# Attention stage of a two-block network: denominators spread through memory, VectorE's convolution taps shared out, the last pair's convolution mostly on TensorE

## The chip, the cores and the metric

The kernel runs on one core of one Trainium2 chip. The core has five engines that run their own queues in order: TensorE (PE, with its weight loads shown as PEld), VectorE (DVE), ScalarE (ACT), GpSimd (POOL) and SyncE (SP), which here only issues DMAs. The metric is device time of one execution in microseconds (us); lower is better. Time before the change: 3925.6 us, the median of 3 runs (3922.62 to 3926.04).

## The reference, cut to what matters

The first block replaces three convolutions by table look-ups with a softmax over 16 centroids; it is not touched by the change. The second block is what the change is about: a group norm, a linear attention with rotary positions, and a depthwise 3x3 convolution ("lepe") that is added to it.

```python
x = relu(L0(x))                      # (32, 1024, 14, 14): look-up convolutions, not touched
y = group_norm(x, G=32)
# _L1_conv_ref(y): 16 heads of 64 channels, n = 14*14
q = elu(Wq @ y[:, :512] + bq) + 1
k = elu(Wk @ y[:, 512:] + bk) + 1
q_rope, k_rope = rope(q), rope(k)
km = k.mean(over n)
z  = 1 / (einsum('bhdn,bhd->bhn', q, km) + 1e-6)          # the denominators
kv = s * s * einsum('bhdn,bhen->bhde', k_rope, y)
attn = einsum('bhdn,bhde->bhne', q_rope, kv) * z
lepe = depthwise_conv3x3(y, lepe_w) + lepe_b
out  = x + attn + lepe
```

## The kernel before, in words

**Stages.** Three look-up layers fill the first 2660 us of the execution. Then the attention stage runs over 16 pairs of images (NP = 16; a pair is 392 positions, N2). All of the change lies in this stage.

**How a pair is worked.** Channels are cut into eight tiles of 128 (c = 0 to 7; half h = 0 is c = 0 to 3, for the queries, h = 1 is c = 4 to 7, for the keys). For each half, `load` brings x and the third layer's output by SP; `front` finishes the first block's output on ACT and DVE (L1124, L1133, L1138) and takes statistics (L1143); `group_norm` averages them on PE (L1165) and makes scales on POOL; `normalise` writes y on ACT, padded to 15 columns so that shifted windows can be read, and then turns x in place into x plus the centre tap and bias of the convolution (both L1218). `channels` multiplies y with the weights on PE (L1250) and makes elu + 1 on ACT (L1259, L1262) and DVE (L1267 queries, L1271 keys). `rope` turns queries and keys on POOL (L1291 to L1298). `tokens` transposes y and keys on PE (L1309) and copies them out on ACT (L1312); `products` makes kv on PE (L1346) and masks it on DVE (L1355).

**Denominators.** `normalisers` makes q times mean k on PE (L1397, 32 columns to each head group) and the inverse z on DVE (L1406, L1407). Then, four times a pair, `normalise_q` spreads four rows of z over 128 partitions with a matmul by a selection matrix (L1418), ACT copies the result to `zb` (L1424), and POOL multiplies the turned queries with it (L1421).

**Output.** For each of four head groups (n = 0 to 3, j = 2, 3, 0, 1; two channel tiles each), `attend` multiplies queries and kv on PE into two PSUM banks `pa` (L1438). `lepe` then adds the eight outer taps of the convolution onto each bank on DVE, one instruction a tap (L1455), and adds the bank onto x (L1469). After two head groups `store` writes a half of the output (L1478). There are eight banks: four `mm`, three `pa`, one `w`.

**Order.** The order of every engine's queue is written out by a planner (`Plan`). Each piece of work is given an engine, a rank (its due time), a weight (its cost in us), what it reads and writes, and a lag until its result can be used. `write` simulates time: an engine that is free takes, of the pieces whose inputs are done and whose buffers are free, the one of lowest rank. The order that comes out is fixed; on the chip an engine waits at a piece whose input is late, and what is behind it waits too. Buffers are `Slot`s that go round in rings in order. The ranks of pair p are offset by t = 80 p, and the attention and taps of a pair are ranked one T = 80 later, so that they fall beside the products of the next pair.

Of the kernel before, what the change touches and what calls it, by code (L numbers as in the profile page):

```python
# [10 lines left out]
F32 = mybir.dt.float32  # L11
# [30 lines left out]
class Slot:  # L42


    def __init__(self, pool, make):
        self.pool, self.make, self.ap, self.left = pool, make, None, 0
# [5 lines left out]
class Plan:  # L52
# [9 lines left out]
    def __init__(self, bufs):  # L62
        self.pieces, self.last, self.read = [], {}, {}
        self.ring = {n: [None] * k for n, k in bufs.items()}
# [19 lines left out]
    def write(self):  # L84
# [9 lines left out]
        nexts = {n: 0 for n in self.ring}  # L94
# [7 lines left out]
        def roomy(slots):  # L102
            take = {}
            for s in slots:
                if s.ap is None:
                    ring = self.ring[s.pool]
                    k = take.get(s.pool, nexts[s.pool])
                    old = ring[k % len(ring)]
                    if old is not None and old.left:
                        return False  # L110
                    take[s.pool] = k + 1
            return True

        while events:
            now, _, done = heapq.heappop(events)
            if done is not None:
                for m in after[done]:
                    count[m] -= 1
                    if count[m] == 0:
                        heapq.heappush(ready[self.pieces[m][0]], (self.pieces[m][1], m))  # L120
                for s in self.pieces[done][5]:
                    s.left -= 1
            if events and events[0][0] <= now:
                continue
            for e in engines:
# [17 lines left out]
                for s in slots:  # L143
                    if s.ap is None:
                        ring = self.ring[s.pool]
                        ring[nexts[s.pool] % len(ring)] = s
                        nexts[s.pool] += 1
                        s.ap = s.make()
# [12 lines left out]
def conv_preact_kernel(ctx: ExitStack, tc: tile.TileContext, a: dict, out: bass.AP):  # L161
# [793 lines left out]
    with ExitStack() as s:  # L955

        once = s.enter_context(tc.tile_pool(name="p4c", bufs=1))
        xp = s.enter_context(tc.tile_pool(name="p4x", bufs=5))
        p2 = s.enter_context(tc.tile_pool(name="p4b", bufs=1))
        mm = s.enter_context(tc.tile_pool(name="ps_mm", bufs=4, space=PSUM))  # L960
        pap = s.enter_context(tc.tile_pool(name="ps_pa", bufs=3, space=PSUM))
        wp = s.enter_context(tc.tile_pool(name="ps_w", bufs=1, space=PSUM))
# [50 lines left out]
        ph = mm.tile([P, 512], F32, tag="mm", name="ph")[:, :P]  # L1013
# [41 lines left out]
        bufs = dict(x=5, o3q=2, e=2, k=2, q=4, qr=5, ks=2, zb=2, mm=4, pa=3, w=1)  # L1055
        bufs |= {f"{n}{h}": 1 for n in ("vt", "kt") for h in range(2)}
        bufs |= {f"kv{i}{jp}": 1 for i in range(2) for jp in range(2)}
        plan = Plan(bufs)
        do = plan.do
        PE, DVE, ACT, POOL, SP = "PE", "DVE", "ACT", "POOL", "SP"  # L1060

        def slot(pool, shape, space=None):
            return Slot(
                pool,
                lambda: (space or p2).tile(shape, F32, tag=pool, name=pool, bufs=bufs[pool]),
            )

        bank = lambda pool: slot(pool, [P, 512], {"mm": mm, "pa": pap, "w": wp}[pool])
# [18 lines left out]
        def load(p, h, rank):  # L1087

            xt = slot("x", [P, 4, N2])
# [12 lines left out]
            for k in range(2):  # L1102
                ot = slot("o3q", [P, 2, N2])
# [9 lines left out]
        def front(p, h, c, xt, ot, rank):  # L1113

            ch = 4 * h + c
            w = bank("w")
# [34 lines left out]
        def group_norm(p, h, rank):  # L1151
# [7 lines left out]
            pm, pv = bank("mm"), bank("mm")  # L1159
# [11 lines left out]
            def centred():  # L1171
                for t in (g("gd"), pd()):
                    nc.vector.tensor_tensor(t, mean, bc(pm()[:, :8], 2, 2), ALU.subtract)
                nc.vector.tensor_tensor(g("gd"), g("gd"), pd(), ALU.mult)
                nc.vector.scalar_tensor_tensor(
                    g("gq"), m2, 1.0 / 98.0, g("gd"), ALU.mult, ALU.add
# [31 lines left out]
        def normalise(p, h, c, xt, rank):  # L1208
# [29 lines left out]
            do(ACT, rank + 24, 0.92, apply("xsc", "xbi", "x"), [key("xsc"), key("xbi")], [xk])  # L1238


        def channels(p, keys, j, r, t, sums, rank):
            w, first, b = (wk, 4, "kb") if keys else (wq, 0, "qb")
            pq, e = bank("mm"), slot("e", [P, N2])
# [33 lines left out]
            do(PE, rank, 2.76, product, ys_, [pq], lag=0.25)  # L1277
# [25 lines left out]
        def tokens(dst, dk, blocks, keys, rank):  # L1303

            pt = bank("mm")
# [5 lines left out]
            do(PE, rank, 0.5, turn, keys, [pt], lag=0.25)  # L1311
# [12 lines left out]
        def k_tokens(p, i, h, jp, kt, rank):  # L1324
# [4 lines left out]
                [("kr", 2 * jp + j) for j in range(2)],  # L1329
# [3 lines left out]
        def products(i, jp, kts, vts, rank):  # L1333

            pk = bank("mm")
            t = slot(f"kv{i}{jp}", [P, 2, 2, P])
# [37 lines left out]
        def normalisers(qs, ks, rank):  # L1374
# [16 lines left out]
            pd = bank("mm")  # L1391
# [16 lines left out]

            qk = [(q, r) for q in qs for r in range(2)]
            do(PE, rank, 2.3, piece, [*qk, ("kmm", 0), ("kmm", 1)], [pd], lag=0.25)  # L1410
            do(DVE, rank - 10, 3.0, inverse, [pd], ["z"])

        def normalise_q(j, qr, rank):
            pz, zb = bank("mm"), slot("zb", [P, N2])
            v = slice(32 * j, 32 * j + 32)

            def spread():
                nc.tensor.matmul(pz()[:, :N2], sel[v], z[v], start=True, stop=True)  # L1418
# [4 lines left out]
            do(PE, rank, 0.6, spread, ["z"], [pz], lag=0.25)  # L1423
            do(ACT, rank - 10, 0.48, lambda: nc.scalar.copy(zb(), pz()[:, :N2]), [pz], [zb])  # L1424
            do(POOL, rank, 1.65, times, [zb], [qr], port=True)

        def attend(j, kvs, qr, rank):


            pa = [bank("pa") for hp in range(2)]  # L1430

            def piece():
                for i in range(2):
                    for r in range(2):
                        for hp in range(2):
# [6 lines left out]
                                start=(r == 0),  # L1442
                                stop=(r == 1),
# [3 lines left out]
            return pa  # L1447

        def lepe(p, c, pa, xt, rank):


            def tap(k):
                def piece():
# [3 lines left out]
                        neighbours(p, c, 15 * (k // 3 - 1) + k % 3 - 1),  # L1457
# [13 lines left out]
            for n, k in enumerate([k for k in range(9) if k != 4]):  # L1471
                do(DVE, rank + n, 0.555, tap(k), [("y", p % 2, c)], [pa])
# [144 lines left out]
```

## Time and profile before

| | us |
|---|---|
| median of 3 runs | 3925.6 |
| profiled execution, its own time | 3921.16 |
| span of that execution | 3919.2 |
| first product of the attention stage (L1250) starts | 2712.5 |
| reciprocals of the denominators (L1407), mean period of the last 11 full pairs before the last | 72.5 |
| last reciprocal starts | 3858.49 |
| PE busy in the span | 3741.2 (95%) |
| DVE busy in the span | 3054.1 (78%) |
| mean granted clock of TensorE | 0.974 |

Each pair repeats the same pattern, so the reciprocal of its denominators marks its period: they start at 2990.17, 3060.87, 3134.89 and so on to 3787.66, and the stretches between them can be compared as windows. In a row of the windows, each engine's busy time stands with the number of its instructions, then the clock granted to TensorE (1 is full speed), and the share and rate of the DMA engines. What is left after the last reciprocal is a tail in which no further pair covers anything.

### The profile page before, as it was taken

The numbers are of one execution on the slowest core, as the hardware profiler recorded it, in microseconds if no ns is written. First come the engines' busy times: TensorE is split into PE (matmuls) and PEld (weight loads), VectorE is DVE, ScalarE is ACT, GpSimd is POOL, SyncE is SP. The second block draws the span as 40 slices with busy tenths as digits, with TensorE's granted clock in tenths as the row PEclk, the third lists the DMA queues.
The fourth block names the chain that finished last, engine by engine and source line by source line (L and its number), as shares of the span: only waits on it lengthen the run. The fifth ranks groups of instructions, "written<-read, shape, count | busy, mean of one in ns | idle before, by whom it ended". The sixth has DMA issues, their size and how long they took to land. (4 is left out here: it accounts for less than half of the span.)

```text
span 3919.2 us, 45921 instructions
## 1 busy us (share of the span) xinstructions
PE 3741.2 (95%) x16475; PEld 2097.3 (54%) x16475; DVE 3054.1 (78%) x4395; ACT 1664.6 (42%) x3797; POOL 2226.9 (57%) x1248
## 2 busy tenths in 40 slices
PE   8999999999999999999999999994999999999995
PEld 5555555544555455554444444442666666666664
DVE  8999999978888888888533333323799999999997
ACT  4555555533333333333222211213756666666661
POOL 7999999964444444444211111103877777777773
PEclk9999999999999999999999999997999999999997
DMA  3111111024333333432011110114122222222111
GB/s 114 34 34 33 34 33 32 2 74 104 83 69 87 69 83 69 97 73 60 32 38 38 38 38 19 38 38 135 42 67 62 71 71 63 67 71 75 55 54 34
DMA packets 209028, 228.13 MB, mean 58 GB/s; under 512 B 23888, under 2 KB 206672, under 8 KB 208792
## 3 DMA queue, kind: packets, MB, share of 16 engines
q1 hardware_dynamic: 208216, 224.96, 21.4%
q8 instruction: 133, 2.18, 0.2%
q14 instruction: 103, 0.84, 0.1%
q10 hardware_dynamic: 576, 0.15, 0.0%
HBM read 151.51 MB, written 73.55 MB: 57 GB/s over the span
## 5 line engine op out<-in xcount | busy, mean ns | idle before, releaser
L525 POOL TENSOR_TENSOR t<-t,r 128x1664 f32<-128x1664 f32 (+1 forms) x284 | 1064.2, 3747 | 1188.8 <-DVE r L524 1153.1
L558 PE MATMUL po<-t,lut 128*128 128x392 f32 x4096 | 1418.4, 500 | 0.5 <-POOL t L525 0.5
L558 PEld LDWEIGHTS po<-t,lut 128*128 128x128 f32 x4096 | 760.0, 190 | 627.0 <-issue 124.7
L487 ACT ACTIVATE t<-sc,cbias 128x392 f32<-128x392 f32 (+1 forms) x1136 | 579.8, 593 | 1034.8 <-PE sc L823 646.9
L1250 PE MATMUL mm<-y,qk 128*128 128x392 f32 x2048 | 727.1, 507 | 4.1 <-POOL xbi L1192 4.1
L909 PE MATMUL po<-t,lut 128*128 128x448 f32 x1792 | 680.3, 540 | 0.0
L499 DVE STREAM_TRANSPOSE tt<-t 128x1664 f32<-128x1664 f32 (+1 forms) x284 | 544.3, 1917 | 168.5 <-ACT t L487 168.5
L1455 DVE SCALAR_TENSOR_TENSOR pa<-y,lepe_w,pa 128x406 f32<-128x406 f32 x1024 | 607.1, 638 | 10.5 <-PE pa L1438 9.2
L524 DVE STREAM_TRANSPOSE r<-rc 128x1664 f32<-128x1664 f32 (+1 forms) x284 | 546.6, 1925 | 21.3 <-DVE rc L518 0.9
L1250 PEld LDWEIGHTS mm<-y,qk 128*128 128x128 f32 x2048 | 386.5, 194 | 283.9 <-issue 32.8
L909 PEld LDWEIGHTS po<-t,lut 128*128 128x128 f32 x1792 | 338.4, 190 | 339.9 <-issue 339.6
L918 DVE BATCH_NORM_STATS2 stats<-o 128x6 f32<-128x448 f32 x112 | 69.0, 617 | 488.4 <-ACT o L917 488.4
L516 DVE TENSOR_REDUCE sm<-tt 128x104 f32<-128x832 f32 (+2 forms) x284 | 423.1, 1490 | 5.4
L502 POOL TENSOR_TENSOR tt<-tt 128x832 f32<-128x832 f32 x128 | 248.1, 1938 | 7.8 <-DVE tt L499 7.8
L917 ACT COPY o<-po 128x448 f32<-128x448 f32 x112 | 59.0, 528 | 419.6 <-PE po L909 375.5
L518 DVE RECIPROCAL rc<-sm 128x104 f32<-128x104 f32 (+1 forms) x284 | 229.5, 808 | 9.8
L814 PE MATMUL sc<-patch,cw 64*128 64x392 f32 x1024 | 211.1, 520 | 4.7 <-DMA patch<-h1d 3.2
L1291 POOL TENSOR_TENSOR kr<-k,cosq 128x784 f32<-128x784 f32 x64 | 104.0, 1625 | 129.8 <-DVE k L1271 100.6
L1421 POOL TENSOR_TENSOR qr<-qr,zb 128x784 f32<-128x784 f32 x64 | 116.1, 1845 | 103.0 <-ACT zb L1424 103.0
L526 ACT ACTIVATE sm<-sm 128x104 f32<-128x104 f32 (+1 forms) x284 | 86.2, 304 | 174.6 <-DVE rc L518 174.6
L1124 ACT ACTIVATE w<-x,tb,gn_a 128x196 f32<-128x196 f32 x256 | 133.3, 521 | 58.5 <-DMA x<-in_x_dram 33.9
L814 PEld LDWEIGHTS sc<-patch,cw 64*128 64x128 f32 x1024 | 90.5, 186 | 116.5 <-issue 73.4
(156 smaller groups left out, 3844.6 us busy)
## 6 DMA issues: line engine op xcount, KB each, us to landing
patch<-h1d SPq DMA_DIRECT2D x248, 162.8 KB
x<-in_x_dram SPq DMA_DIRECT2D x32, 784.0 KB
o3d<-o SPq DMA_DIRECT2D x14, 1792.0 KB
x<-in_x_dram SPq DMA_DIRECT2D x64, 392.0 KB
o3q<-o3d SPq DMA_DIRECT2D x64, 392.0 KB
out_dram<-x SPq DMA_DIRECT2D x64, 392.0 KB
h1d<-pad SPq DMA_DIRECT2D x96, 225.0 KB
patch<-h1d SPq DMA_DIRECT2D x124, 108.5 KB
```

The lines of the kernel that those rows point to most:

```text
L487: nc.scalar.activation(t[:, j, : sc.shape[1]], sc, AF.Identity if exact else AF.Exp, bias=bias[:, j : j + 1],)
L499: nc.vector.transpose(tt, tf)
L502: nc.gpsimd.tensor_tensor(tv[:, :, :8], tv[:, :, :8], tv[:, :, 8:], ALU.add)
L516: nc.vector.tensor_reduce(sm, tv, AX.X, ALU.add)
L518: nc.vector.reciprocal(rc, sm)
L524: nc.vector.transpose(r, bc(rc, 2, KC))
L525: nc.gpsimd.tensor_tensor(tf, tf, r, ALU.mult)
L558: nc.tensor.matmul(po[h], luts[b][:, j, h * P : (h + 1) * P], ts[u % len(ts)][:, j, :N2], start=(b == 0 and j == 0), stop=(b == 7 and j == 3),
L814: nc.tensor.matmul(sc, w8[r, 8 * h + 4 * (j // 2) + g], grid(pbuf[n % NPB][r, j // 2, g]), start=True, stop=False,)
L909: nc.tensor.matmul(po, luts[g][:, m * P : (m + 1) * P], t3[h][:, g % 4, :], start=(g == 0), stop=(g == 7),)
L1250: nc.tensor.matmul(pv(), w[kt][:, m0 : m0 + P], ywin(p, first + kt), start=(kt == 0), stop=(kt == 3),)
L1455: nc.vector.scalar_tensor_tensor(acc, neighbours(p, c, 15 * (k // 3 - 1) + k % 3 - 1), lw[:, c, k : k + 1], acc, ALU.mult, ALU.add,)
```

## The change

It does these things:

- In all pairs but the last, z is written to a buffer in device memory by SP (`keep`), and four DMAs read it back with each row repeated over 32 partitions into `zb` (`spread`). The selection matmul and the ACT copy stay for the last pair alone. `zb` has four buffers in place of two.
- One outer tap of each of the four tiles c = 4 to 7 (three of every tile in the last pair) leaves DVE: ACT scales the shifted y into a buffer (`shifted`) and POOL adds it onto x (`onto`).
- The due times of DVE's taps are 1.5 apart in a tile, and the tiles of a group start 12 apart and groups 18 apart, so that taps of two tiles are due alternately.
- In the last pair, for three of the four head groups, the remaining five taps of each tile are matmuls on PE: ACT makes a diagonal matrix of the tap's weights in the memory of the key weights (which are no longer needed), PE multiplies the shifted y with it into the bank, and `attend` then accumulates onto that. The banks of these groups come from `pa`, `mm` and `w`.
- The planner's buffers are allocated once and taken from a list of free ones instead of in ring order, and the due times are gathered in a table with new values.

```diff
-        self.ring = {n: [None] * k for n, k in bufs.items()}
+        self.free = {n: list(ts) for n, ts in tiles.items()}
...
         def roomy(slots):
...
+            take = [s.pool for s in slots if s.ap is None]
+            return all(take.count(n) <= len(self.free[n]) for n in take)
...
+                    if s.left == 0:
+                        self.free[s.pool].append(s.ap)
...
+                        s.ap = self.free[s.pool].pop(0)
...
+        for n, k in (("zb", 4), ("e", 2)):
+            ring(n, k, [P, N2])
+        ring("side", 2, [P, 2, 14, 14])
...
+            held = [("held", j // 2)] if keys else []
+            done = ["wk"] if keys and p == NP - 1 else []
+            do(PE, rank, 2.76, product, ys_ + done, [pq, *held], lag=0.25)
...
+            def keep():
+                nc.sync.dma_start(zd[p % 2], z)
+
             qk = [(q, r) for q in qs for r in range(2)]
             do(PE, rank, 2.3, piece, [*qk, ("kmm", 0), ("kmm", 1)], [pd], lag=0.25)
-            do(DVE, rank - 10, 3.0, inverse, [pd], ["z"])
+            do(DVE, rank - 10, 3.1, inverse, [pd], ["z"])
+            if p < NP - 1:
+                do(SP, rank - 10, 0.45, keep, ["z"], [("zd", p % 2)], lag=2.5)
...
             def spread():
+                nc.sync.dma_start(zb(), bc(zd[p % 2, 32 * j : 32 * j + 4], 1, 32))
+
+            def select():
                 nc.tensor.matmul(pz()[:, :N2], sel[v], z[v], start=True, stop=True)
...
+            if p < NP - 1:
+                do(SP, rank - 10, 0.58, spread, [("zd", p % 2)], [zb], lag=5.0 + 1.7 * n)
+            else:
+                do(PE, rank, 0.6, select, ["z"], [pz], lag=0.25)
+                do(ACT, rank - 10, 0.48, lambda: nc.scalar.copy(zb(), pz()[:, :N2]), [pz], [zb])
             do(POOL, rank, 1.65, times, [zb], [qr], port=True)
...
-                                start=(r == 0),
-                                stop=(r == 1),
+                                start=(r == 0 and not onto),
+                                stop=(r == 1 and (i == 1 or not onto)),
...
-            for n, k in enumerate([k for k in range(9) if k != 4]):
-                do(DVE, rank + n, 0.555, tap(k), [("y", p % 2, c)], [pa])
-            do(DVE, rank + 8, 0.48, added, [pa], [(xt, c % 4)])
+            for k in mine:
+                do(DVE, rank, 0.545, tap(k), [("y", p % 2, c)], [pa])
+                rank += due["tap"]
+            do(DVE, rank, 0.48, added, [pa], [(xt, c % 4)])
+
+        def side_tap(p, c, k, xt, rank):
...
+            def shifted():
+                off = LEAD + offset(k)
+                v = ys[p % 2][:, c, off : off + 2 * IMG]
+                nc.scalar.activation(
+                    side(),
+                    v.rearrange("p (i r c) -> p i r c", r=15, c=15)[:, :, :14, :14],
+                    AF.Copy,
+                    scale=lw[:, c, k : k + 1],
+                )
+
+            def onto():
+                nc.gpsimd.tensor_tensor(
+                    xc(), xc(), side().rearrange("p i r c -> p (i r c)"), ALU.add
+                )
+
+            do(ACT, rank - 6, 0.52, shifted, [("y", p % 2, c)], [side])
+            do(POOL, rank - 4, 1.02, onto, [side], [(xt, c % 4)], port=True)
+
+        diagonals = iter([t[:, P * n : P * n + P] for t in wk for n in range(C // P)])
+
+        def diagonal_taps(p, c, ks, pa, rank):
+            for n, k in enumerate(ks):
+                dg = next(diagonals)
+
+                def diagonal(k=k, dg=dg):
+                    nc.scalar.activation(dg, ident, AF.Copy, scale=lw[:, c, k : k + 1])
+
+                def piece(n=n, k=k, dg=dg):
+                    nc.tensor.matmul(
+                        pa()[:, :406],
+                        dg,
+                        neighbours(p, c, offset(k)),
+                        start=(n == 0),
+                        stop=False,
+                    )
+
+                do(ACT, rank, 0.3, diagonal, [], ["wk", ("dg", c, k)])
+                do(PE, rank, 0.68, piece, [("dg", c, k), ("y", p % 2, c)], [pa], lag=0.25)
...
+        due = dict(
...
+            rope_q=55,
...
+            v1=69,
...
+            k1=62,
+            kv0=55,
+            kv1=72,
+            den=60,
+            scaled=45,
+            attend=72.5,
+            sums=20,
+            lepe=86,
+            taps=9.0,
+            half=12.0,
+            tap=1.5,
+            side=103,
+            diagonal=105,
+        )
...
-            normalisers(qs, ks, t + 68)
+            normalisers(p, qs, ks, at["den"] - (10 if p == NP - 1 else 0))
...
+            last = p == NP - 1
+            pools = {0: "pa pa", 1: "mm mm", 2: "pa w", 3: "mm mm"} if last else {}
             for n, j in enumerate(js):
-                pa = attend(j, kvs, qrs[j], t + T + 2.5 + 19 * n)
+                pa = [Slot(b) for b in pools.get(n, "pa pa").split()]
+                by_pe = last and n < 3
+                taps = {}
                 for hp in range(2):
                     c = 2 * j + hp
-                    lepe(p, c, pa[hp], xts[c // 4], t + T + 2.0 + 9.5 * (2 * n + hp))
+                    taps[c] = [k for k in range(9) if k != 4]
+                    for m in range(3 if last else c // 4):
+                        r = at["side"] + due["taps"] * 2 * n + due["half"] * hp
+                        side_tap(p, c, taps[c].pop(1), xts[c // 4], r)
+                    if by_pe:
+                        diagonal_taps(p, c, taps[c], pa[hp], at["diagonal"] + n)
+                        taps[c] = []
+                attend(j, kvs, qrs[j], pa, at["attend"] + due["sums"] * n, by_pe)
+                for hp in range(2):
+                    c = 2 * j + hp
+                    r = at["lepe"] + due["taps"] * 2 * n + due["half"] * hp
+                    lepe(p, c, pa[hp], xts[c // 4], taps[c], r)
```

## The prediction

> **What bounds the kernel now.** I read the page's busy rows, then windows cut at each pair's reciprocal, then one pair's timeline by engine, then the waits, then the tail. Two regular periods (clock 1.00 and 0.95), the last full one and the tail; columns are the stretch, its length, PE, PEld, DVE, ACT, POOL busy (instructions), granted clock, DMA share, GB/s:
>
> ```profile
> 3498.28:3568.94 70.66, 69.43 (x445) 47.32 (x442) 69.54 (x164) 47.64 (x100) 53.48 (x48) 1.00 0.23 69
> 3641.27:3715.29 74.02, 72.78 (x446) 48.74 (x442) 69.63 (x165) 47.76 (x100) 53.52 (x48) 0.95 0.22 66
> 3787.66:3858.49 70.83, 69.74 (x431) 46.51 (x428) 60.58 (x136) 34.38 (x70) 50.89 (x42) 0.98 0.07 24
> 3858.49:3919.20 60.71, 16.96 (x110) 13.43 (x106) 46.01 (x80) 1.85 (x4) 7.24 (x4) 0.57 0.13 40
> ```
>
> See three things. PE and DVE are both full, within 1.2 us of the period; POOL has 17 us free and ACT 23. A period lengthens with the clock alone: DVE's and POOL's work is the same in both rows, PE's grows by 3.35. And the tail is 60.7 us in which DVE works alone.
>
> Where PE's missing 1.2 us lie, by PE's, DVE's and POOL's timelines of the pair whose reciprocal starts at 3353.59:
>
> ```profile
> 3353.59 2.60 DVE L1407 RECIPROCAL z<-z 128x392 f32<-128x392 f32 x1
> ...
> 3356.34 2.39 PE L1418 MATMUL mm<-z,hsel 32*128 32x392 f32 x8 [0.99 <-DVE z L1407]
> 3358.66 7.23 PE L1250 MATMUL mm<-y,qk 128*128 128x392 f32 x16
> ...
> 3357.84 7.26 POOL L1421 TENSOR_TENSOR qr<-qr,zb 128x784 f32<-128x784 f32 x4 [6.73 <-ACT zb L1424]
> ```
>
> PE waits 0.99 for the reciprocal, spends 2.39 on selection, and its next 16 products take 7.23 where 32 of them take 10.78 elsewhere: half clock. The windows of the next pair's spot say when:
>
> ```profile
> 3417.90:3422.60 4.70, 4.55 (x46) 4.00 (x46) 4.70 (x12) 4.67 (x11) 4.54 (x5) 1.00 0.31 82
> 3422.60:3428.00 5.40, 5.12 (x97) 4.35 (x96) 5.37 (x8) 2.16 (x5) 0.88 (x1) 1.00 0.02 6
> 3428.00:3430.60 2.60, 1.80 (x7) 0.91 (x8) 2.60 (x6) 0.96 (x3) 0.40 (x1) 1.00 0.00 0
> 3430.60:3434.10 3.50, 3.50 (x7) 1.51 (x6) 3.50 (x10) 1.56 (x4) 3.50 (x3) 0.51 0.19 35
> ```
>
> The clock halves right after the wait and selection (third row), and for 3.5 us. The tail, on DVE:
>
> ```profile
> 3867.71 8.87 DVE L1455 SCALAR_TENSOR_TENSOR pa<-y,lepe_w,pa 128x406 f32<-128x406 f32 x16 [2.62 <-PE pa L1438]
> ...
> 3903.66 8.95 DVE L1455 SCALAR_TENSOR_TENSOR pa<-y,lepe_w,pa 128x406 f32<-128x406 f32 x16 [2.12 <-PE pa L1438]
> 3912.52 1.04 DVE L1469 TENSOR_TENSOR x<-pa,x 128x392 f32<-128x392 f32 x2
> ```
>
> Four groups of 12.0 us each (taps, adds, and 2.12 until PE has refilled the banks), then 5.6 us of store.
>
> **The change, part by part.** *Denominators, PE.* Four selections leave: 2.39 us, and the wait of 0.99. I take 3.4 off PE. The clock: the last 11 periods before the last pair average 72.5, against 70.66 unthrottled: 1.84 a pair. The row gives the cause: 1 us of wait and a few narrow matmuls. Here the Trainium skill (TensorE: Matmul & The Clock Gate, "Part 1: The HAM clock gate") speaks against counting this: it asks for an idle window of about 3.4 us before the clock halves, so a 1 us wait would cost 1 us; and its "Part 4: PE-mode transpose" says that transposes do not count as busy in the same way, so the stretch of transposes that stays would throttle anyway. By these rules the 1.84 stays. By the rows, the transposes (first row) run at 1.00 and the drop follows the selection. I go by the rows, but not fully: new gaps may do the same, so I count 1.35 of the 1.84 as gained.
>
> *Denominators, the new path.* Five DMAs a pair on SP's queue. Transfers of 200 KB are not in the trace; by those of 392 KB, the SP issue takes 0.37 to 0.5, and the trace's landing marks put the last mark 3.15 us after issue for a load (3285.91 to 3289.06) and 2.95 for a store (3295.21 to 3298.16). Half the size: about 2.3 for the write, 2.5 for the first read, 0.9 for each further: the first `zb` some 5 us after z, the last at 8. Bounds: 4 (fixed part alone) and 10 (each at the full 3 us, reads overlapping little). Before, POOL's first multiplication came 1.6 us after z's end; now some 3.4 later, and the last waits until 8 after z at the earliest. POOL already idles 6.7 at this spot and has the turning of the next keys to do first; the planner allows 8.5 us and puts other work there. On SP, `keep` waits for z and `spread` for the write to land: behind them are loads of the next pair and the stores, which issue every 4 to 14 us; 2 to 3 us late there is covered by buffers (x has 5), except the third layer's output (2 buffers): 3420.03 issued, 3422.93 landed, used at 3424.83, 1.9 us of cover; its cost if gone is 1 to 2 us of DVE in a pair. I take 0.
>
> *Taps moved.* DVE starts tap after tap every 0.547 us (8 in 4.46). Four a pair: 2.2 off DVE. ACT: four copies `zb` of 0.49 go, four of 0.52 (by its 392-element passes, 0.53) come: +0.1. POOL: four adds of 1.02 (as L1298): +4.1, to 57.6 of some 68; covered by its 17 us of idle. If that cover goes, POOL still is 10 us from being the bound.
>
> *Alternation.* In 11 pairs, 22 taps and 22 final adds start 0.67 after the tap before them instead of 0.547; the rest already alternate or do not wait. At most 44 x 0.13 / 11 = 0.5 us of DVE a pair.
>
> *Sum a pair.* PE needs 69.43 - 2.39 = 67.0. DVE: issue intervals of a pair add up to 68.3 (64 taps 34.9; products' passes and sums 9.8; front 12.4; final adds 3.8; kv 2.4; z 3.1; small ones 1.9), plus 0.5 of stalls; less 2.2 is 66.1 to 66.6. Both at 67 leaves little slack; I allow 1.0 of waits for each other: 68.0, and 0.5 of clock left: 68.5. From 72.2 (2775 to 3858.5, 15 periods) that is 3.7 x 15 = 56 us. Buffers from a free list: cost 0 (they only widen the planner's choice; bound 1 us a pair either way, there being no row for it).
>
> *Tail.* PE had finished the last pair's kv at 3860.5. It now has, in addition, 30 diagonal taps (two matmuls each; 8 products take 2.65, scaled to 406 columns 0.69 a tap): 20.6 us, and the four attentions at 1.57: 6.3; less the previous pair's selection 2.4: PE done at 3885. ACT makes 30 diagonals (0.3, a 128-element pass; 0.2 to 0.5) and 24 shifted copies: 22 us, within the 36 us it has free in that period. POOL gets 28 adds, 28.6 us: 50.9 + 28.6 + 7.2 = 87 from 3790, so 3877, beside PE. DVE then has ten taps and two adds for the last group: 6.5; store 5.6. End: 3897 instead of 3919: 22 us. If PE is at half clock there, the diagonals take 41 us and nothing is gained; the diagonals themselves keep PE fed, so I take full clock.
>
> *Sum.* 56 + 22 = 78. The profiled execution, whose own time was 3921.16, would come to 3843; the median of the runs was 4.4 above it, so 3848.
>
> **Rivals.** *Half of it* (0.22): clock drops stay (the skill's reading) and only PE's 3.4 or a part comes, DVE being level with it: period 70.3, 28 us, tail 20: 3878. For: 1 us sufficed to halve the clock. Against: transposes at 1.00.
>
> *The tail stays* (0.12): PE goes to half clock, or POOL's 28 adds and four multiplications end last (they cannot start until x and y are there): only the 56 us: 3870.
>
> *Slower: PE waits for the scaled queries* (0.06). `attend` is in PE's fixed order; behind it are the next pair's products, for which ACT, DVE and POOL wait in turn. If `zb` comes late, PE waits w for L1421, and the clock halves for one or two windows (+3.4 at worst). The period is 67.0 + w + 3.4. Against the gain of the tail, 22/15 = 1.5 a pair, it decides from w = 72.2 + 1.5 - 70.4 = 3.3 us. At w = 5: 75.4, +48 - 22: 3952. Against: before, the first attention came 10 us after z's end (3366.16), with its multiplication done in 3.5; the DMAs' 5 and a multiplication of 1.85 fit into that.
>
> *It does not do what it says:* the alternation has at most the 0.5 us above to give; its whole worth is inside the range.
>
> **How the numbers follow.** The forecast, both gains, has 0.58. Its range, 3826 to 3868, is from a period of 67.5 and a tail of 28 (-99) to 69.5 and 17 (-57). The rivals of 3870 and 3878 add 0.34; with their bounds (71 a period, tail 10: -28) they reach 3898. I give 3822 to 3890, leaving out the slower case and the ends. About 0.2% (8 us) is what can be told from no change here; the cases put 0.02 inside it, 0.06 beyond it on the slow side, 0.92 on the fast.
>
> **What would show it.** Right: no L1418 wait but in the last pair; periods between reciprocals near 68.5 with PE and DVE over 97% busy; the half-clock window gone from most pairs; 60 taps on DVE a pair; POOL near 57; the tail after the last reciprocal near 40 us at a clock near 1. Wrong: PE idle before the attentions with POOL's L1421 as releaser, DVE idle on the third layer's output, or the diagonals at double length.

## The result, and the profile after

The changed kernel takes 3863.58 us (median of 4 runs, 3857.28 to 3866.39); the kernel before, on the same chip, took 3925.24 us. The ratio is 0.9842, with a 95% interval of 0.9825 to 0.9859. The time moved by 61.7 us, to the faster side; the forecast was 78, its range held. The profiled execution took 3857.28 us for a span of 3855.4, at a mean granted clock of 0.986.

The spans of the two profiled executions differ by 63.8 us, and fall into three parts:

| | before | after | difference | forecast |
|---|---|---|---|---|
| start to the first product of the stage (not touched) | 2712.5 | 2709.9 | -2.6 | 0 |
| first product to the end of the last pair's last product | 1133.5 | 1091.5 | -42.0 | -56 |
| from there to the end | 73.2 | 54.0 | -19.3 | -22 |

First the windows between reciprocals of the changed kernel: two regular periods, the last one, and what is left after the last reciprocal. The columns are those of the windows shown before.

```profile
2975.48:3044.07 68.59, 67.52 (x432) 45.92 (x432) 66.83 (x159) 47.05 (x99) 57.38 (x53) 1.00 0.30 86
3253.66:3322.47 68.81, 67.46 (x432) 45.80 (x432) 66.03 (x159) 48.03 (x101) 57.45 (x53) 1.00 0.29 86
...
3743.12:3819.54 76.42, 74.71 (x503) 50.88 (x504) 67.63 (x148) 54.63 (x123) 72.63 (x65) 1.00 0.14 46
3819.54:3855.40 35.86, 26.08 (x123) 14.91 (x121) 12.14 (x19) 1.75 (x4) 7.26 (x4) 0.90 0.14 45
```

A regular period is down to 68.6 to 68.8 us at full clock. VectorE (third busy column) fell by 3 us and GpSimd rose to 57.4. In the last period PE does 503 matmuls where it did 431: work that stood behind the last reciprocal, eleven diagonal products among it, now stands ahead of it. So the tail after the last reciprocal, 60.7 us before and 35.9 now, overstates the gain; the table above compares it from the last product. The reciprocals of the changed kernel come 65 to 76 us apart, because their place in the order shifts from pair to pair; by its first products a pair takes 69.0 us, and took 72.0. That is 46 us over fifteen pairs; the last pair's own products take 4.3 longer (57.3 where it was 53.0). Stretches of half clock before the last reciprocal fell from 51.2 us in twelve pieces to 3.4 us in one.

The spot at which PE had waited for the reciprocal, by the timelines of PE, DVE, POOL and SP's queue:

```profile
3253.66 2.60 DVE L1410 RECIPROCAL z<-z 128x392 f32<-128x392 f32 x1
...
3255.39 1.14 PE L1312 MATMUL mm<-ident,y 128*105 128x128 f32 x8
3256.29 0.34 SPq L1413 DMA_DIRECT2D zd<-z  x1
3256.36 2.80 PE L1250 MATMUL mm<-y,qk 128*128 128x392 f32 x8
...
3258.25 2.35 SPq L1429 DMA_DIRECT2D zb<-zd  x4
...
3264.47 1.84 POOL L1435 TENSOR_TENSOR qr<-qr,zb 128x784 f32<-128x784 f32 x1 [4.61 <-DMA zb<-zd]
...
3268.64 1.65 PE L1454 MATMUL pa<-qr,kv 64*128 64x210 f32 x16
```

No PE instruction waits for z itself any more. The write is issued 0.03 us after z's end (3256.26), the four reads, which wait for it to land, from 2.0 later, and POOL's first multiplication starts 8.2 us after z's end. POOL pays for the way through memory with 4.6 us of idle, and that idle is cover: the first attention comes without a wait. What PE waits for instead is in the waits of eleven pairs (2975.48 to 3743.12; total, times, longest):

```profile
POOL qr L1435 <- DMA zb<-zd: 46.2, 16, 6.4
...
PE mm L1312 <- ACT kt L1315: 11.0, 6, 2.4
```

The second row is new: transposes that wait for ScalarE's copies of the turned keys, 1.0 us a pair. And the tail, on PE and then on DVE:

```profile
3828.51 4.36 PE L1528 MATMUL mm<-y,qk 128*128 128x406 f32 x12
...
3840.72 1.64 PE L1454 MATMUL mm<-qr,kv 64*128 64x210 f32 x16
3842.29 2.31 PE L1528 MATMUL w<-y,qk 128*128 128x406 f32 x6
...
3842.46 4.48 DVE L1472 SCALAR_TENSOR_TENSOR mm<-y,lepe_w,mm 128x406 f32<-128x406 f32 x8 [3.46 <-PE mm L1454]
...
3848.89 1.03 DVE L1486 TENSOR_TENSOR x<-mm,x 128x392 f32<-128x392 f32 x2
```

PE now sets the end, up to 3842.36: its diagonals run there at 0.68 us a tap (two matmuls, from start to start), and DVE waits 3.46 us for the attention of the group that keeps its taps on DVE. From then on DVE works without a gap, ten taps and four additions onto x to 3849.9, and 5.5 us of store remain. PE's last diagonals (to 3844.6) and last attention (to 3846.2) end while DVE is still at its taps.

### The profile page after: what moved, and what is told of

The parts are those of the page before. It is cut to its first block, busy times and chain, and to the rows that moved or that the text cites. A ratio compares the mean times of both kernels' runs of the same rounds, so it can differ in the third digit from the quotient of the medians.

```text
span 3855.4 us, 45891 instructions
## 1 busy us (share of the span) xinstructions
PE 3706.0 (96%) x16415; PEld 2070.7 (54%) x16415; DVE 2992.6 (78%) x4281; ACT 1688.2 (44%) x3851; POOL 2308.7 (60%) x1332
## 5 line engine op out<-in xcount | busy, mean ns | idle before, releaser
L1250 PE MATMUL mm<-y,qk 128*128 128x392 f32 x2048 | 717.1, 496 | 6.9 <-POOL xbi L1192 4.1
L1472 DVE SCALAR_TENSOR_TENSOR pa<-y,lepe_w,pa 128x406 f32<-128x406 f32 x900 | 537.7, 637 | 8.9 <-PE pa L1454 6.1
L1250 PEld LDWEIGHTS mm<-y,qk 128*128 128x128 f32 x2048 | 371.9, 189 | 255.7 <-issue 11.4
L804 PEld LDWEIGHTS sc<-patch,cw 64*128 64x128 f32 x1024 | 90.7, 186 | 115.7 <-issue 73.2
L1262 ACT ACTIVATE e<-e 128x392 f32<-128x392 f32 x256 | 135.4, 529 | 3.3
```

The source lines that it names most:

```text
L804: nc.tensor.matmul(sc, w8[r, 8 * h + 4 * (j // 2) + g], grid(pbuf[n % NPB][r, j // 2, g]), start=True, stop=False,)
L1250: nc.tensor.matmul(pv(), w[kt][:, m0 : m0 + P], ywin(p, first + kt), start=(kt == 0), stop=(kt == 3),)
L1472: nc.vector.scalar_tensor_tensor(acc, neighbours(p, c, offset(k)), lw[:, c, k : k + 1], acc, ALU.mult, ALU.add,)
```

## The experiments

Medians in us; "before" is the kernel before on the same chip.

| kernel | median | before | ratio, 95% interval |
|---|---|---|---|
| before with the way through memory alone (e1_dma_only) | 3920.85 | 3921.79 | 0.9996 [0.9987, 1.0005] |
| changed, selection kept in all pairs (e2_select_kept) | 3877.59 | 3921.79 | 0.9886 [0.987, 0.9903] |
| changed, no taps on GpSimd in the first 15 pairs (e3_no_side) | 3859.36 | 3921.79 | 0.9841 [0.9825, 0.9858] |
| changed, last pair like the others (e4_no_diag) | 3873.51 | 3921.79 | 0.9875 [0.9858, 0.9891] |
| changed, due times of the taps as before (e5_taps_in_turn) | 3850.03 | 3923.38 | 0.9813 [0.9795, 0.9831] |
| before, reciprocal's lag raised (e6_z_late) | 3960.27 | 3923.38 | 1.0097 [1.0077, 1.0116] |
| changed, without memory way, side taps, diagonals (e9_order_only) | 3902.03 | 3923.38 | 0.9944 [0.9926, 0.9962] |
| changed, group norm's product in SBUF (e10_gd_sbuf) | 3869.24 | 3923.38 | 0.9862 [0.9844, 0.988] |
| the changed kernel again (after_again) | 3857.28 | 3924.95 | 0.9834 [0.9817, 0.985] |
| e5 without side taps in the first 15 pairs (e11_turn_no_side) | 3858.98 | 3924.95 | 0.9832 [0.9815, 0.9848] |
| e5 with two key buffers (e12_turn_two_kt) | 3859.29 | 3924.95 | 0.9833 [0.9816, 0.9849] |
| e9 with the taps' old due times (e13_order_turn) | 3903.19 | 3924.95 | 0.9943 [0.9927, 0.996] |

**A caution on small differences.** The two profiles of the changed kernel come from identical source, and yet GpSimd's instructions of the stage, of which there are some 860 in both, stand in another order at 347 places. The planner visits engines by a loop over a Python set of their names (`engines = {p[0] for p in self.pieces}`), whose order is not fixed from one build to the next, so two pieces that are free at once can be taken either way. This is read from the code; no run held the order fixed. The eight runs of the changed kernel lie between 3855 and 3866 us. A difference under some 10 us between two single variants is therefore not assigned to their edit below.

**The way through memory alone.** Into the kernel before go `zb` with four buffers, the buffer in device memory, and the two kinds of DMA for all pairs but the last:

```diff
+            if p < NP - 1:
+                do(SP, rank - 10, 0.45, keep, ["z"], [("zd", p % 2)], lag=2.5)
...
+            if p < NP - 1:
+                do(SP, rank - 10, 0.58, fetch, [("zd", p % 2)], [zb], lag=5.0 + 1.7 * n)
```

> The kernel before with the denominators' way through memory alone (zb with four buffers, five DMAs a pair, selection kept for the last pair); nothing else of the change. Theory 'PE bound': PE loses 2.4 of selection, the 1.0 wait and the 1.8 of half clock a pair, and DVE (68.3 of issue intervals) is then the next bound at about 69.5: some 2.7 x 15 = 40 us faster, 3885. Rival 'DVE level': DVE takes over at once, period 70.7, only the clock's loss comes back: 27 us or less, 3898 or above. Rival 'late zb': attentions wait, PE idles before them and the clock still halves: 3920 or above.

It gave nothing, 0.9 us. By its number that fits both rivals, so PE's waits have to decide. Below stand a stretch of eleven pairs in the kernel before and then in this one, the shares of the span in the chain of work that ended last, in the same order, and PE's longest waits in this kernel over the stretch:

```profile
2990.00:3787.00 797.00, 783.18 (x4834) 528.88 (x4832) 765.22 (x1804) 524.95 (x1100) 588.56 (x528) 0.97 0.23 67
2990.00:3787.00 797.00, 752.51 (x4665) 504.91 (x4662) 780.85 (x1793) 506.76 (x1044) 584.89 (x525) 0.99 0.27 81
...
PE 17%; DVE 9%; ACT 3%; POOL 1%; issue 1%; DMA 0%; SPq 0%; DVEq 0%; POOLq 0%; ACTq 0%
DVE 18%; PE 4%; POOL 4%; ACT 2%; issue 2%; DMA 1%; SPq 0%; DVEq 0%; POOLq 0%; ACTq 0%
...
PE mm L1309 <- DVE kv L1355: 11.3, 14, 1.5
PE mm L1165 <- DVE nmc L1178: 10.8, 14, 1.5
PE mm L1250 <- ACT vt L1312: 8.9, 8, 1.9
```

PE's work fell, from 71.2 to 69.0 us a pair in the mean of eleven periods between reciprocals, and half clock in the pairs fell from 51.2 to 13.7 us. But DVE's rose from 69.6 to 71.6 with the same instructions, and the chain now runs over DVE. Of PE's 44 us of waits 30 are for DVE and none is for the multiplication with `zb`, which rules out the late `zb`. Where DVE's time grew, the groups of DVE show (count, then busy us, mean ns); first the kernel before over eleven pairs, then this one over the same stretch:

```profile
L1175 DVE SCALAR_TENSOR_TENSOR gq<-gst,gd 128x16 f32<-128x16 f32 x22 | 9.1, 415 | 0.8
L1379 DVE TENSOR_TENSOR kmm<-ks,hmean 128x32 f32<-128x32 f32 x22 | 5.3, 239 | 0.0
```

```profile
L1175 DVE SCALAR_TENSOR_TENSOR gq<-gst,gd 128x16 f32<-128x16 f32 x22 | 21.8, 992 | 0.8
L1379 DVE TENSOR_TENSOR kmm<-ks,hmean 128x32 f32<-128x32 f32 x22 | 20.9, 962 | 0.0
```

Two tiny instructions, 16 and 32 elements wide, took a microsecond each: 28.3 us more over eleven pairs, 2.6 a pair, which is the whole growth of DVE and more. They are the ones with both inputs in SBUF. One of them, beside GpSimd and PE:

```profile
3187.58 1.71 POOL L1292 TENSOR_TENSOR ru<-q,sinq 128x784 f32<-128x784 f32 x1
...
3188.46 0.86 DVE L1175 SCALAR_TENSOR_TENSOR gq<-gst,gd 128x16 f32<-128x16 f32 x1
...
3189.46 0.58 PE L1165 MATMUL mm<-gq,gavg 128*128 128x8 f32 x4 [1.49 <-DVE nmc L1178]
```

It starts while GpSimd's instruction runs and ends 0.03 us after it (3189.32 and 3189.29); PE then waits 1.49 us for the DVE instruction behind it. It is so throughout: in the fourteen traces of this case 305 instructions of these two kinds took over 0.3 us, and 300 of them ended 0.03 to 0.06 us after the GpSimd instruction that ran when they began. The Trainium skill (SBUF — State Buffer, "Who interferes with whom") says that a VectorE instruction with two SBUF inputs contends with a GpSimd instruction that reads SBUF; this trace agrees. GpSimd's instructions here last 1 to 1.9 us, and with the new order the two meet them more often: 57 of 64 took over 0.3 us in this trace, 20 of 64 before. So DVE, which had stood level with PE, became the bound, and PE's gain alone buys nothing. The way through memory with these two instructions cured was not run, so what PE's gain would then have bought is not shown.

**The selection kept.** In the changed kernel both tests for the last pair are made false, so all pairs use the matmul and ScalarE's copy.

```diff
-            if p < NP - 1:
+            if False:
```

> The changed kernel with the selection matmul and the ACT copy in all pairs, no DMA of the denominators; all else as changed. Theory: PE has 2.4 more a pair and waits for the reciprocal again; if the clock's halving goes with that, 2.4 + 1.0 + 1.8 = 5.2 a pair at most, and 15 pairs make 50 to 75 us slower than the changed kernel: 3915 to 3935. Rival 'order': the new due times put other work between the reciprocal and the selection, so that PE does not wait and the clock stays: only the 2.4 come back, 36 us, 3900.

44.2 us faster than before without the memory way, and faster than either expectation had it. A regular period and PE's timeline:

```profile
3125.87:3196.62 70.75, 69.38 (x443) 47.06 (x441) 68.10 (x161) 49.55 (x105) 57.72 (x54) 1.00 0.24 69
```

```profile
3057.34 0.65 PE L1312 MATMUL mm<-ident,y 128*105 128x128 f32 x4
3058.11 1.58 PE L1432 MATMUL mm<-z,hsel 32*128 32x392 f32 x8
3059.66 0.69 PE L1312 MATMUL mm<-ident,y 128*105 128x128 f32 x4
3060.28 3.71 PE L1349 MATMUL mm<-vt,kt 105*64 105x128 f32 x64
```

The selection stands between transposes, waits for nothing, takes 1.58 us where 2.39 had been charged to it, and the clock stays whole (3.4 us of half clock in all). So the drops had not come from the selection as such, but from how it stood. This new order is nearly without them, selection or not (not every one is: see e13_order_turn below). What the memory way adds on top is 3877.59 less the changed kernel's 3857 to 3864: 14 to 20 us. PE is busy 1.9 us less in a pair (69.4 to 67.5), which would be 28 us over 15 pairs; the rest comes back as PE's waits, whose idle goes from 1.3 to 1.7 a pair, and as smaller disturbances of the period.

**No side taps.** `range(3 if last else c // 4)` becomes `range(3 if last else 0)`.

> The changed kernel with no tap moved off DVE in the first 15 pairs (the last pair as changed). Theory 'PE bound': DVE goes from 66 to 68.3 of a period of 69.1, PE still has 67.5: between 0 and 1.5 a pair, 0 to 20 us slower, 3863 to 3885. Rival 'DVE bound': the whole 2.2 a pair comes back, 33 us: 3896.

The same as the changed kernel. A period, and the shares of the span in the chain that ended last, in the changed kernel and then in this one:

```profile
3116.68:3185.87 69.19, 67.59 (x431) 45.59 (x431) 68.88 (x163) 46.17 (x96) 53.49 (x49) 1.00 0.30 85
...
PE 12%; DVE 10%; ACT 3%; POOL 2%; DMA 2%; issue 1%; SPq 0%; DVEq 0%; POOLq 0%; ACTq 0%
DVE 20%; PE 3%; ACT 2%; POOL 2%; issue 2%; DMA 1%; SPq 0%; DVEq 0%; POOLq 0%; ACTq 0%
```

DVE is full, 68.9 of 69.2, and the chain runs over it. With the side taps DVE is 66 to 67 busy in such a period, the chain is shared with PE, and the period is no shorter: PE's 67.5 of work and its waits take 69 as well. PE and DVE stand at nearly the same height, and lowering one of them alone gives nothing.

**The last pair like the others.** `pools = {}`, `by_pe = False` and `range(c // 4)` for all pairs.

> The changed kernel with its last pair as all others (one tap of c = 4 to 7 on POOL, all the rest on DVE, banks from pa; no diagonals). Theory: the time after the last product returns to the 73 us of before, less the 2 us of the four taps on POOL: 17 to 20 us slower than the changed kernel, 3881 to 3883; PE half-clocked in the tail. Rival: the earlier denominators of the last pair give most of it: under 8 us slower, 3871.

The windows of the last full period and of the tail after the last reciprocal:

```profile
3747.29:3811.35 64.06, 63.48 (x397) 41.84 (x397) 58.66 (x133) 32.10 (x65) 51.69 (x44) 1.00 0.13 42
3811.35:3872.50 61.15, 20.70 (x170) 16.91 (x168) 47.76 (x83) 5.75 (x12) 8.71 (x6) 0.62 0.12 40
```

10 to 16 us slower than the changed kernel, and by the two profiles all of it lies behind the last product: 68.0 us where the changed kernel has 54.0. The tail is again DVE's, 47.8 us busy in 61.2 with PE mostly idle at clock 0.62; the diagonals trade it for PE's work at full clock.

**Order alone.** e2's kernel with e4's two settings and `range(0)` for the side taps: what stays of the change are the planner's new due times (the last pair's denominators 10 earlier than the others' among them), buffers from a free list, four `zb`, and the group norm's product in PSUM. The earlier due time and the product in PSUM are part of the change, though its description above does not list them.

> The changed kernel without its three moves of work: selection matmul and ACT copy in all pairs, no tap on POOL, no diagonals. What is left of the change is the new due times, the free list of buffers and the group norm's product kept in PSUM. Theory 'order': the moves of work do not matter in the pairs; what counts is that the new order puts transposes and the kv products between the reciprocal and the selection, so PE no longer waits and its clock no longer halves: 1.0 + 1.8 a pair, 15 pairs, 35 to 45 us faster than before, 3878 to 3890, with no half clock in the pairs. Rival 'work': with DVE at 68.3 and PE at 69 again nothing or little is gained, 3910 or above.

```profile
3126.88:3198.35 71.47, 69.38 (x440) 46.98 (x440) 70.28 (x164) 47.55 (x101) 53.65 (x48) 1.00 0.23 69
```

21.4 us faster with no operation removed, and no half clock before the last reciprocal. That is less than the 35 to 45 expected of the order, and more than the rival's little or nothing. The period, 71.47, is 2.1 over PE's busy time and 1.2 over DVE's. From here to e2's kernel, side taps and diagonals bring 24 us: behind the last product, where the diagonals work, 70.3 us become 53.4, and the pairs' part falls by 6.1. The period falls from 71.5 to 70.7, so the side taps may be worth something while the selection stays and DVE is at 70 us, and nothing measurable without the selection. The 6 us are within the caution above, and why they should differ is not shown: both kernels without side taps leave DVE 0.3 to 1.5 us of slack, and PE's waits differ.

**The product in PSUM.** In the changed kernel, `centred` writes the product to `gd` in SBUF again, and `gq` reads it there.

```diff
-                nc.vector.tensor_tensor(pd(), g("gd"), pd(), ALU.mult)
+                nc.vector.tensor_tensor(g("gd"), g("gd"), pd(), ALU.mult)
...
-                    g("gq"), m2, 1.0 / 98.0, pd(), ALU.mult, ALU.add
+                    g("gq"), m2, 1.0 / 98.0, g("gd"), ALU.mult, ALU.add
```

> The changed kernel with the group norm's product written to SBUF again, as before the change (two instructions a half). In the kernel before, the instruction that reads it (L1175, two inputs in SBUF) took 0.47 us in the mean and the next one came up to 0.57 later; with PSUM it takes 0.18. Theory 'port': it waits for POOL's instruction in progress, which POOL's four more adds make likelier: 0.5 to 1.2 of DVE a pair and the queue behind it; as PE is the bound, 0 to 10 us slower than the changed kernel. Rival: no difference in the instruction's time, the 0.47 were something else.

The one instruction over eleven pairs, in the changed kernel and then in this one:

```profile
L1175 DVE SCALAR_TENSOR_TENSOR gq<-gst,mm 128x16 f32<-128x16 f32 x22 | 3.8, 175 | 0.8
```

```profile
L1175 DVE SCALAR_TENSOR_TENSOR gq<-gst,gd 128x16 f32<-128x16 f32 x22 | 17.5, 797 | 0.8
```

175 against 797 ns for the same 16 elements: with one input in PSUM it does not wait for GpSimd. In the ten traces that have it so, it began 251 times of 320 while a GpSimd instruction ran, and never took over 0.182 us. That is 1.2 us a pair of DVE; the time is 6 to 12 us worse, near the limit of what the orders' spread lets one say, and this kernel also has 10.2 us of half clock in the pairs where the changed kernel's two profiles have 3.4 and 6.8. The duration is shown, the share in the time is not.

**Taps in turn.** The taps get the due times of before (`lepe=82, taps=9.5, half=9.5, tap=1.0`), by which two tiles do not alternate.

> The changed kernel with the old due times of DVE's taps (1.0 apart, tiles 9.5 apart, from 82) and nothing else changed. The changed kernel shows 5.4 starts of a tap on its own tile's last tap a pair at 0.67 us where before had 2.0, so the alternation did not lessen these. Theory 'no effect': within 8 us of the changed kernel, 3855 to 3870. Rival 'alternation pays': slower by over 15 us, DVE busier by over 1 us a pair.

```profile
3253.43:3322.50 69.07, 67.40 (x432) 45.90 (x432) 67.52 (x161) 48.14 (x101) 57.97 (x53) 1.00 0.29 85
3322.50:3390.94 68.44, 67.52 (x432) 46.09 (x432) 66.72 (x159) 47.74 (x101) 56.78 (x53) 1.00 0.30 86
```

The fastest of all: its four runs, 3849.34 to 3851.27, lie under all eight of the changed kernel, and it beats both kernels. Its periods are regular and it has no half clock before the last reciprocal. So the alternation was not seen to pay. It does not even do what it is for: taps and adds that start some 0.67 us after the tap before instead of 0.547 number 44 in eleven pairs before the change, 65 in the changed kernel and 66 in this one, 0.5 us a pair and then 0.8. Since the changed kernel and this one have as many, the gain over the changed kernel does not come from them; whether it is more than a luckier order is open.

**Four follow-ups.** e11_turn_no_side is e5 with e3's edit; e12_turn_two_kt is e5 with two key buffers and their due time at 52 in place of 62; e13_order_turn is e9 with e5's edit; after_again is the changed kernel once more, as an anchor on their chip.

> The changed kernel itself, beside the runs that follow, as their anchor: 3857 to 3867, as in its four runs so far; no or one stretch of half clock in the pairs.

> The changed kernel with the old due times of the taps (as in the kernel that took 3850.0) and no tap moved off DVE in the first 15 pairs. With the new due times the taps on POOL were worth nothing (3859.4 without them). Theory 'PE bound either way': 3845 to 3856. Rival 'the stalls ate it': once DVE has less stalls the 2.2 us a pair count: 3865 or above.

> The changed kernel with the old due times of the taps, two buffers for the transposed keys in place of one, and the second image's key transposes due 10 earlier, so that they stand between query products and not in a row. Theory: PE's last regular wait, 14.4 us in 11 pairs on ACT's copies of the transposes, comes from eight transposes in a row (0.44 to 0.49 each on PE, a copy starting every 0.46 to 0.48 on ACT, four banks); spread out, 1.0 to 1.3 a pair goes, 15 us: 3835. Rival 'DVE follows': DVE at 66.9 of 68.9 becomes the bound and 3845 to 3850 stays.

> The kernel with the new order alone (selection in all pairs, no tap on POOL, no diagonals: 3902.0), with the taps' old due times. There DVE was busy 69.8 of 71.5 with 9.0 taps a pair that start 0.67 after the tap before on the same tile (before: 2.0). Theory 'stalls': with half of these gone DVE gets 0.5 to 0.8 a pair back and the time falls by 8 to 15 us: 3888 to 3894. Rival: within 4 us of 3902; then DVE is bound by its work.

None moved the time beyond the caution above, and the gains hoped for in e12 (to 3835) and e13 (to 3888 to 3894) did not come. In e12 the waits for the key copies went and others, for the value copies, came (8.5 us, 9 times); PE idled 1.6 us a pair where e5 idles 1.3. In e13 the taps that start late behind the tap before did fall, from 9.0 to 5.7 a pair, but half clock came back, 20.5 us in the pairs, so the one may have paid for the other. e11 was to tell whether the side taps matter once the taps are in turn: it has 13.7 us of half clock, e5 has none, and it settles nothing.

**A late reciprocal.** The planner is told that z comes later, so as to move the selection behind other work of PE: `do(DVE, rank - 10, 3.0, inverse, [pd], ["z"], lag=2.0)` in the kernel before.

> The kernel before with one number changed: the planner is told that the reciprocal's result comes 2.0 us after its end instead of 0.12, so that it puts products of the next pair between reciprocal and selection. Work is the same, only PE's wait at that place goes. Theory 'the wait halves the clock': no half clock in the pairs (51 us of it before), 1.0 + 1.8 a pair: 3890 +- 10. Rival 'narrow matmuls halve it': the clock still halves in most pairs, only the wait of 1.0 goes, 3910; rival 'DVE level': the clock stays up but DVE (68.3 and stalls) cannot follow: 3905 or above with PE idle elsewhere.

It failed as a cure: 36.9 us slower. PE's timeline and three windows at the spot:

```profile
3378.61 1.14 PE L1418 MATMUL mm<-z,hsel 32*128 32x392 f32 x2 [1.43 <-ACT zb L1424]
3380.97 0.99 PE L1165 MATMUL mm<-gst,gavg 128*128 128x8 f32 x4 [1.23 <-DVE gst L1143]
```

```profile
3375.80:3379.20 3.40, 1.97 (x10) 0.60 (x8) 3.40 (x9) 2.56 (x6) 0.57 (x1) 1.00 0.00 0
3379.20:3382.60 3.40, 2.17 (x6) 1.36 (x6) 3.30 (x13) 0.94 (x3) 3.40 (x3) 0.50 0.44 125
3382.60:3386.00 3.40, 3.40 (x7) 1.80 (x6) 3.33 (x5) 0.19 (x1) 3.28 (x2) 0.50 0.00 0
```

The wait moved into the selection, a second one followed, and each of the two windows is followed by 3.4 us at half clock: 95.6 us in fourteen pairs, against 51.2. At half speed these 44 us more cost at most 22. The rest has other causes, and one of them shows in the trace: the two tiny DVE instructions of e1, L1175 and L1379, took 38.5 us over the stretch from 2990 to 3787, where they took 14.4 in the kernel before.

## Why the prediction was right or wrong

- **Direction and size.** Faster by 61.7 where 78 was forecast, inside the range. The term that was mis-sized is the pairs' 56, which measured 42: a pair took 69.0 where 68.5 was forecast, from 72.0 and not 72.2, and the last pair's products took 4.3 longer, which was not priced. The tail's 22 measured 19.
- **PE's 67.0 a pair** measured 67.5 in the regular periods. The 2.39 charged to the selection was too much: PE is busy 69.38 a pair with it (e2, e9) and 67.5 without, so it was 1.9.
- **"I allow 1.0 of waits for each other"**: PE idles 1.7 a pair on average (1.1 to 1.4 in the windows shown). The new wait is that of transposes for ScalarE's key copies, 1.0 a pair alone, which the prediction did not name.
- **The clock.** 1.35 of 1.84 was counted; nearly all came. The rows were a better guide than the rule: in these traces a window with 1 us of wait and a few narrow matmuls was enough to halve the clock, and transposes ran at 1.00: in e1 a window of the clock with nothing but transposes (from 3128.94, 2.96 us busy) is followed by full clock. But the step's reason was only half of it. It gave the gain to the removed selection, and in e1 the removal does take half clock from 51.2 to 13.7 us; yet e2 and e9 keep the selection and have 3.4 and none in their pairs, through the order alone, which leaves PE no wait ahead of the narrow matmuls. In the changed kernel both are at work, and their shares were not separated.
- **The way through memory** cost no wait that the trace shows on PE, as forecast: in the pair shown the first `zb` took 8.2 us after z's end, not 5, but inside the bounds of 4 to 10, and POOL's idle took it. PE's weight loads for the attention waited at most 0.6 us for POOL's multiplication, so the slower rival had nothing to stand on.
- **Four taps to GpSimd** did take DVE down and GpSimd to 57.6 a pair, as forecast, at 1.02 us an add and 0.63 a shifted copy (0.52 forecast). Their worth in time was nothing (e3): PE and its waits stood as high.
- **Alternation** was given at most 0.5 us a pair; no gain was seen (e5, e13).
- **The group norm's product in PSUM** was not priced at all. It lowers one DVE instruction from 0.80 to 0.18 us, and the time that such instructions take when they meet GpSimd is what undid the memory way alone (e1). If e10's difference is its doing, which is not shown, the forecast would have missed by 6 to 12 us more without it.
- **The tail.** PE's diagonals ran at full clock at 0.68, with 0.69 estimated; from the last product to PE's last attention took 44.8 us where 39 was forecast, and what follows 9.2 where 12.1 was. The two errors cancel in part: DVE did not wait for the end of PE's work, as the sum had it, but started its last taps 3.7 us ahead of that. The rival in which GpSimd's adds end last is out: they were done at 3814.8, its multiplications at 3831.8.

The gains do not add up by part. Memory way alone: 1; on top of the rest: 14 to 20. Order, free list and PSUM product: 21. Diagonals: 10 to 16. Side taps: nothing with everything else in place. Which of the ingredients of order-alone brings its 21 us was not separated beyond the PSUM product's 6 to 12. The profiled executions, cut as in the first table, show where each step works:

| | first product to the last product's end | from there to the end |
|---|---|---|
| before | 1133.5 | 73.2 |
| memory way alone (e1) | 1133.6 | 72.7 |
| order, free list, PSUM product (e9) | 1116.3 | 70.3 |
| and side taps and diagonals (e2) | 1110.2 | 53.4 |
| and the memory way: the changed kernel | 1091.5 | 54.0 |
| the changed kernel without diagonals (e4) | 1092.7 | 68.0 |

## What to carry to other kernels

Where two engines stand within a microsecond or two of the period, relieving one of them buys little (1 us here) until the other is relieved too; try each edit alone and each edit left out before crediting it. A short wait of the matrix engine next to narrow matmuls can cost more than itself, since 3.4 us of half clock followed it here; independent work in that spot cured it in one order (e2, e9) and made it worse in another (e6), so read the clock again after each new order. A tiny VectorE instruction that waits for GpSimd counts as busy in the profile and shows by its length alone (0.17 against 0.86 us here), so compare the mean length of a group between two kernels. And before comparing variants of a kernel whose order a program writes, make that program's order reproducible.

## What was not expected of the hardware

**The clock drops on a partly busy window.** The kernel before, on the same grid of 3.4 us (first window, the one after it, and one of another pair that had no drop):

```profile
3355.50:3358.90 3.40, 2.46 (x9) 1.16 (x10) 3.40 (x8) 1.59 (x4) 1.06 (x1) 1.00 0.00 0
3358.90:3362.30 3.40, 3.40 (x6) 1.72 (x6) 3.40 (x8) 1.19 (x3) 3.40 (x3) 0.51 0.38 99
...
3498.90:3502.30 3.40, 2.41 (x28) 1.51 (x24) 3.40 (x4) 0.35 (x1) 0.00 (x0) 1.00 0.00 0
```

PE was busy 2.46 of 3.40 us and the clock was halved for the next window; the Trainium skill (TensorE: Matmul & The Clock Gate, "Part 1: The HAM clock gate") asks for an idle window of that length. Another window with 2.41 busy was not followed by a drop, so busy time alone does not decide; nor does the number of matmuls, 9 and 28 here, since a window with 25 (from 3280.44) was followed by a drop. All fourteen traces, cut from 2780 to 3840 us into the clock's own windows, have 4279 windows at full clock, 50 of them followed by a drop. The best cut by busy time misplaces 34 of the 4279; by busy time weighted with each matmul's share of the 128 rows (the selection has 32), the best cut, near 1.5 us, misplaces 10. So narrow matmuls probably count for less; no run varies the rows by themselves. The lengths fit the page's 3.413 us window that does not follow the kernel: the period of e6 settles at 75.09 us, which is 22.0 of them.

**Tiny VectorE instructions wait for GpSimd.** With both inputs in SBUF, an instruction on 16 elements took 0.42 us in the mean of the kernel before, 0.80 in e10 and 0.99 in e1, by how often it met GpSimd, and 0.175 with one input in PSUM.
